# A search of three bits a step, two dense tiles and scattered results in a layer of experts that choose

## The chip, the cores and the metric

The kernel runs on one core of one Trainium2 chip. A core has a matrix engine (TensorE, PE in the profile, with its weight loads as PEld), a vector engine (VectorE, DVE), an activation engine (ScalarE, ACT), a general engine (GpSimd, POOL), and a synchronisation engine (SyncE, SP) that issues most DMAs; ACT and POOL issue DMAs too. Each engine works through its own queue in order, and queues wait for each other by semaphores. The metric is device time in microseconds (us). Three runs of the kernel before took 3548.22, 3555.48 and 3563.23; the median is 3555.48.

## The reference

A decoder of four levels, each with an attention, a cross attention with a context and a feed-forward part, works on x, 2048 tokens (16 batches of 128) of 256 values. Every part is `x = x + part(layernorm(x))`. The change touches the feed-forward part of level 2, in which 8 experts choose their tokens, and the end of the loop that three cross attentions share.

```python
def _L2_ffn_ref(x, Wg, W1, W2):          # E = 8, T = 2048, cap = T // E = 256
    logits = xt @ Wg
    probs = jax.nn.softmax(logits, axis=-1)
    pT = probs.T
    _, top_idx = jax.lax.top_k(pT, cap)
    sel = jnp.zeros((E, T), dtype=bool).at[jnp.arange(E)[:, None], top_idx].set(True)
    masked = jnp.where(sel, pT, -jnp.inf)
    assigned = sel.any(axis=0)
    tok2exp = jnp.where(assigned, jnp.argmax(masked, axis=0), jnp.argmax(pT, axis=0))
    weights = jnp.take_along_axis(probs, tok2exp[:, None], axis=1)[:, 0]
    out = jnp.zeros_like(xt)
    for e in range(E):
        gate = jnp.where(tok2exp == e, weights, 0.0)
        h = jax.nn.gelu(xt @ W1[e], approximate=False) @ W2[e]
        out = out + gate[:, None] * h
    return out.reshape(B, S, D)
```

Each expert takes its 256 likeliest tokens; a token goes to the likeliest of the experts that took it, or, if none did, to the likeliest of all. So every token has exactly one expert, and the number of an expert's tokens depends on the data. W1[e] is 256x512 and W2[e] 512x256, 512 KB each.

## The kernel before

x lies in SBUF as 16 tiles of 128 tokens, four groups of four (`self.x[g][:, t, :]`). The parts run one after the other. A list scheduler places most instructions; those that go through `pinned`, `pinned_transpose` (L255 to L260) or `keep_in_program_order` keep the order in which the program states them on PE. So PE's order around the change is written by hand. PSUM tiles come from `b1` (one bank, four buffers) and `b2` (two banks, two buffers).

**Cross attention** (`xattn64`, for L1, L2 and L3). Its loop (L1230 to L1248) is a pipeline over units, 16 of them in L2. Turn m runs the sums d of unit m-1, the scores st of unit m, the values o of unit m-1, whose normalising product rb (PE) is copied by ACT (L1213) and multiplied in by DVE into cT (L1215), and then the output projection of unit m-2 (`project`, L1218), which `add_x` (L222) adds to x. Level 2 hands in a dictionary `beside` of work for single turns: it comes from `l2_ffn_begin` (L1850 to L1912), which also prepares DRAM rows and SBUF tiles. From turn 10 on it lays the statistics, the normalised rows ("hall") and the logits of group after group beside the attention. The logits of a group are two products per half with the gate weights wg as the stationary operand, 32 columns of which 8 are used, and 512 tokens moving ("lT", 32x512). The work of the last group (`st["last"]`) is left for `l2_ffn`.

**Experts** (`l2_ffn`, L1914 to L2168). In order:

- tail: group 3's statistics, rows, transposes, logits; the lT of all groups is turned back, softmax over 8 logits gives p (128x16x8), one transpose gives pT, 128x128, in which partition (tile, expert) holds 128 tokens' probabilities;
- search (L1994 to L2003): the 256th largest probability of each expert, as the bits of a float32, two bits in each of 15 steps. DVE makes three candidates, compares pT with each in an instruction that also sums its mask, PE adds up over the 16 partitions of an expert ("count"), DVE keeps the largest candidate that at least 256 tokens reach;
- ranks (`ranks`, L2008 to L2017): which tokens are above or at the threshold, each token's expert, its place `at` among the expert's tokens (L2071), the expert of every block of 128 places (`ebi`). Experts fill up to 16 + 7 = 23 blocks, each with tokens of one expert;
- moves (L2086 to L2093): 16 indirect DMAs by POOL write the rows of a tile to their places in DRAM `hs`, which was filled with zeros long before;
- blocks (L2150 to L2161): 23 blocks, two stages deep. `fetch` (L2098) reads rows (ACT's queue, after the moves; block 0 alone, then four at once) and, on SP, the block's weights by a register that holds the expert; weights use one of 7 slots of 8 KB per partition that the whole program shares (`slot`, L118). `tokens` transposes the rows ("htr"), `first_product` (tokens stationary, 512 columns of W1 moving, then gelu on ACT), `turn` transposes the result ("ytr", DVE copy), `second_product` (256 columns of W2 moving), whose result yo (two buffers) ACT copies and sends to DRAM `ys`;
- return (L2162 to L2168): 16 indirect DMAs by POOL gather each token's row of ys, and DVE adds it, times the gate, to x.

Then `l3_attn` (L2172) begins with the layernorm of group 0.

Of the kernel before, what the change touches and what calls it, by code (L numbers as in the profile page):

```python
# [17 lines left out]
P = 128  # L18
B = 16
# [11 lines left out]
class Decoder:  # L31
# [1052 lines left out]
    def xattn64(self, H, names, bias, tag, begin=None):  # L1084
# [12 lines left out]
        with self.tc.tile_pool(name=tag, bufs=1) as wk:  # L1097
# [132 lines left out]
            for m in range(N + 2):  # L1230
                if 0 < m <= N:
                    r = sums(es[m - 1])
# [10 lines left out]
                if m > 1:  # L1243
                    project(*units[m - 2], cTs.pop(m - 2))
# [605 lines left out]
    def l2_ffn_begin(self):  # L1850


        nc = self.nc
        E = 8
        wg = self.wp.tile([P, 2, 32], F, tag="wg2", name="wg2")
        nc.gpsimd.memset(wg, 0.0)
        nc.sync.dma_start(out=wg[:, :, 0:E], in_=self.a["L2_ffn_Wg"].rearrange("(c p) n -> p c n", p=P))
        zero = self.hp.tile([P, DM], F, tag="hT", name="zero", bufs=5)
        nc.gpsimd.memset(zero, 0.0)
        NB = B + E - 1  # L1860
        hs = self.tc.dram_tile([NB * P, DM], F, name="hs")
        for b in range(NB):
            nc.sync.dma_start(out=hs[b * P : (b + 1) * P, :], in_=zero)
        h = [self.slot([P, 8, DM], "hall") for _ in range(2)]
        st = {"hs": hs, "h": h}
        self.l2f = st
        vals = {}

        def stats(gs):
            n = len(gs)  # L1870
            bs = self.small([P, GB, 6], "bnst")
            mv = self.small([P, n, GB, 2], "l1mv")
            rs = self.small([P, n, GB], "l1rs")
            for i, g in enumerate(gs):
                for t in range(GB):
                    nc.vector.bn_stats(bs[:, t, :], self.x[g][:, t, :])
                    nc.vector.bn_aggr(mv[:, i, t, :], bs[:, t, :])
            self.rsqrt(rs, mv[:, :, :, 1])
            for i, g in enumerate(gs):
                vals[g] = mv[:, i], rs[:, i]  # L1880

        def rows(g):
            mv, rs = vals[g]
            for t in range(GB):
                nc.vector.tensor_scalar(
                    h[g // 2][:, g % 2 * GB + t, :], self.x[g][:, t, :], mv[:, t, 0:1], rs[:, t : t + 1], ALU.subtract, ALU.mult
                )

        def logits(g):
            hT = self.hp.tile([P, 2, GT], F, tag="hT", name="hT", bufs=5)  # L1890
            for k in range(2):
                ps = self.b1("tr")
                for t in range(GB):
                    self.pinned_transpose(ps[:, t * P : (t + 1) * P], h[g // 2][:, g % 2 * GB + t, k * P : (k + 1) * P])
                self.evac(hT[:, k, :], ps)
            r = slice(32 * g, 32 * g + 32)
            ps = self.b1("lT")
            for k in range(2):
                self.pinned(ps[r, :], wg[:, k, :], hT[:, k, :], start=k == 0, stop=k == 1)
            if g == 0:  # L1900
                st["lT"] = self.hp.tile([P, GT], F, tag="h", name="lT", bufs=2)
            nc.scalar.copy(st["lT"][r, :], ps[r, :])

        st["last"] = [lambda: stats([3]), lambda: rows(3), lambda: logits(3)]
        at = lambda f, *a: lambda: f(*a)
        return {
            10: [at(stats, [0, 1]), at(rows, 0)],
            11: [at(rows, 1), at(logits, 0)],
            12: [at(logits, 1)],
            14: [at(stats, [2]), at(rows, 2)],  # L1910
            15: [at(logits, 2)],
        }  # L1912

    def l2_ffn(self):  # L1914

        nc = self.nc
        E, CAP = 8, T // 8
        NB = B + E - 1  # L1920
# [3 lines left out]
        with self.tc.tile_pool(name="l2f", bufs=1) as wk:  # L1924
# [7 lines left out]
            for i in range(15):  # L1932
                for j in range(3):
                    nc.gpsimd.memset(bits[:, i, j : j + 1], (j + 1) << (2 * i))
# [738 lines left out]
```

## Time and profile before

| what | value |
|---|---|
| median of three runs | 3555.48 us |
| profiled execution | 3552.78 us, span 3551.1 us |
| PE busy | 3291.6 us (93%), 20930 instructions |
| DVE busy | 2121.4 us (60%) |
| ACT busy | 1416.5 us (40%) |
| POOL busy | 418.6 us (12%) |
| mean granted PE clock | 0.967 |
| chain that ended last | PE 79%, DVE 10%, ACT 5%, issue 3% |
| weights of blocks, 46 DMAs of 512 KB | 5.0 us from issue to landing |

Everything in the profile is one execution. Its page divides the span in 40 equal slices of 88.8 us; a digit is a busy share in tenths, and "PEclk" is the clock that the throttle granted to PE, in tenths of full speed. The windows of the trace give the same for chosen stretches: busy time of each engine with the number of instructions in parentheses, the clock, the share of the 16 DMA engines, and GB/s. A timeline line has start, duration, engine, line of the program, operation, output<-input with shapes, how many were taken together, and in brackets the idle time before and what ended it. "ACTq" and "SPq" are DMA issues on these queues. "at+5" below means 5 us after the cast that makes `at` ended (2246.4).

### The profile page before, as it was taken

The numbers are of one execution on the slowest core, as the hardware profiler recorded it, in microseconds if no ns is written. First come the engines' busy times: TensorE is split into PE (matmuls) and PEld (weight loads), VectorE is DVE, ScalarE is ACT, GpSimd is POOL, SyncE is SP. The second block draws the span as 40 slices with busy tenths as digits, with TensorE's granted clock in tenths as the row PEclk, the third lists the DMA queues.
The fourth block names the chain that finished last, engine by engine and source line by source line (L and its number), as shares of the span: only waits on it lengthen the run. The fifth ranks groups of instructions, "written<-read, shape, count | busy, mean of one in ns | idle before, by whom it ended". The sixth has DMA issues, their size and how long they took to land.

```text
span 3551.1 us, 51415 instructions
## 1 busy us (share of the span) xinstructions
PE 3291.6 (93%) x20930; PEld 1776.4 (50%) x20947; DVE 2121.4 (60%) x4215; ACT 1416.5 (40%) x1896; POOL 418.6 (12%) x603
## 2 busy tenths in 40 slices
PE   7999999999999999998999997478999999999999
PEld 4656655555566566664555564352222222225656
DVE  5546444444565545477777544336999989954430
ACT  2357111111124322247555222024677767783221
POOL 5410000000003310110000210113000000002100
PEclk9989999999999999999999998687999999999989
DMA  2000000000010100010100000655102020000000
GB/s 79 1 23 15 18 18 18 22 19 18 29 50 2 38 1 1 1 43 13 42 1 13 2 1 1 216 177 135 25 12 32 12 32 11 11 1 26 1 8 18
DMA packets 90500, 105.46 MB, mean 30 GB/s; under 512 B 11380, under 2 KB 72694, under 8 KB 90006
## 3 DMA queue, kind: packets, MB, share of 16 engines
q1 hardware_dynamic: 79672, 89.71, 9.8%
q0 software_dynamic: 4224, 6.43, 0.6%
q10 hardware_dynamic: 6368, 6.03, 0.5%
q8 instruction: 165, 2.70, 0.3%
q14 instruction: 71, 0.58, 0.1%
HBM read 85.53 MB, written 16.60 MB: 29 GB/s over the span
## 4 chain that ended last, share of the span: by engine, by line
PE 79%; DVE 10%; ACT 5%; issue 3%; DMA 1%; POOL 1%; POOLq 0%; DVEq 0%; ACTq 0%
PE acc L2205 7%; PE down L257 7%; PE gate L257 6%; PE up L257 6%; PE proj L257 6%; PE st L2205 5%; PE one L2205 4%; PE st L257 4%; PE qT L168 4%; PE h L257 2%; PE o L257 2%; DVE mx L2351 2%; PE rb L257 2%; PE v L1113 2%; PE fc L168 2%
## 5 line engine op out<-in xcount | busy, mean ns | idle before, releaser
L2351 DVE TENSOR_REDUCE mx<-one 128x1 f32<-128x512 f32 x1024 | 658.4, 686 | 59.0 <-PE one L2205 50.0
L2488 ACT ACTIVATE e<-st 128x1024 f32<-128x1024 f32 x512 | 497.1, 1021 | 209.6 <-PE st L2205 208.5
L803 ACT ACTIVATE gs<-gate,cols 128x512 f32<-128x512 f32 x132 | 90.7, 687 | 551.3 <-PE gate L257 544.3
L2205 PE MATMUL acc<-e,v 128*32 128x512 f32 x2048 | 285.6, 612 | 0.9 <-ACT e L2488 0.9
L817 DVE SCALAR_TENSOR_TENSOR x<-down,w_all,x 128x256 f32<-128x256 f32 x512 | 212.4, 477 | 110.4 <-PE down L257 110.2
L2205 PE MATMUL st<-qp,kp 113*128 113x512 bf16 x1024 | 272.4, 386 | 6.0 <-DMA qp<-shifts 3.7
L257 PE MATMUL down<-expert,gs 128*128 128x256 f32 x1056 | 249.4, 379 | 2.2 <-DVE gs L804 2.2
L257 PE MATMUL gate<-hT,expert 128*128 128x512 f32 x528 | 248.5, 593 | 0.2 <-ACT hT L712 0.2
L257 PE MATMUL up<-hT,expert 128*128 128x512 f32 x528 | 248.1, 592 | 0.0
L257 PEld LDWEIGHTS down<-expert,gs 128*128 128x128 f32 x1056 | 200.6, 190 | 85.7 <-issue 61.5
L804 DVE SCALAR_TENSOR_TENSOR gs<-up,cols,gs 128x512 f32<-128x512 f32 x132 | 99.0, 750 | 228.6 <-PE up L257 227.7
L2205 PE MATMUL one<-kp,qp 16*128 16x512 bf16 x1024 | 211.3, 396 | 3.7 <-DVE mx L2351 2.4
L2205 PEld LDWEIGHTS <-qp 16*128 16x128 bf16 x1024 | 48.8, 91 | 327.4 <-issue 322.1
L257 PEld LDWEIGHTS up<-hT,expert 128*128 128x128 f32 x528 | 100.3, 190 | 126.3 <-issue 126.3
L2205 PEld LDWEIGHTS <-kp 113*128 113x128 bf16 x1024 | 79.0, 98 | 143.9 <-issue 82.5
L1213 ACT COPY rb<-rb 128x512 f32<-128x512 f32 x64 | 37.5, 585 | 259.7 <-PE rb L257 259.7
L1215 DVE TENSOR_TENSOR cT<-o,rb 128x512 f32<-128x512 f32 x64 | 44.2, 691 | 151.8 <-ACT rb L1213 151.8
L257 PEld LDWEIGHTS gate<-hT,expert 128*128 128x128 f32 x528 | 99.6, 190 | 70.3 <-issue 63.5
L168 PE MATMUL qT<-hT,L_xattn_Wq 128*128 128x512 f32 x256 | 114.1, 599 | 4.8 <-DVE hT L112 4.8
L257 PE MATMUL o<-e,v 128*32 128x128 f32 (+1 forms) x2048 | 104.6, 277 | 12.6 <-DVE nm L294 11.8
L1524 DVE SCALAR_TENSOR_TENSOR xs<-xBC,cols,xs 128x508 f32<-128x508 f32 x144 | 106.0, 741 | 12.3 <-ACT xs L1520 9.0
L257 PEld LDWEIGHTS o<-e,v 128*32 128x32 f32 (+1 forms) x2048 | 80.9, 123 | 28.4 <-POOL e L335 12.3
(539 smaller groups left out, 5371.2 us busy)
## 6 DMA issues: line engine op xcount, KB each, us to landing
W<-in_L_ffn_W_dram SPq DMA_DIRECT2D x46, 512.0 KB, 5.0
expert<-in_L_ffn_Wg_dram SPq DMA_DIRECT2D x32, 128.0 KB, 2.2
expert<-in_L_ffn_Wu_dram SPq DMA_DIRECT2D x32, 128.0 KB, 2.4
expert<-in_L_ffn_Wd_dram SPq DMA_DIRECT2D x32, 128.0 KB, 2.4
parts<-parts SPq DMA_DIRECT2D x16, 256.0 KB, 2.4
qp<-parts SPq DMA_DIRECT2D x28, 128.0 KB, 3.8
kp<-parts SPq DMA_DIRECT2D x12, 256.0 KB, 8.3
hs<-zero SPq DMA_DIRECT2D x23, 128.0 KB, 1.9
```

The source lines that it names most:

```text
L168: self.nc.tensor.matmul(out, lhsT, rhs, start=i == 0, stop=i == n - 1 and bias is None)
L257: self.tc.keep_in_program_order(self.nc.tensor.matmul(*a, **k))
L803: nc.scalar.activation(gs, pg, AF.Silu, bias=bg)
L804: nc.vector.scalar_tensor_tensor(gs, pu, bu, gs, ALU.add, ALU.mult)
L817: nc.vector.scalar_tensor_tensor(xt, pd[:, t, :], w_all[:, o : o + 1], xt, ALU.mult, ALU.add)
L1113: nc.tensor.matmul(ps, l, r, start=True, stop=False)
L1213: nc.scalar.copy(rb, ps)
L1215: nc.vector.tensor_tensor(cT, po, rb, ALU.mult)
L1524: stt = lambda *a: pin(nc.vector.scalar_tensor_tensor(*a))
L2205: self.tc.keep_in_program_order(nc.tensor.matmul(*a, **k))
L2351: nc.vector.tensor_reduce(mx[:, t, kc, i : i + 1], pair[i], AX.X, ALU.max)
L2488: nc.scalar.activation(e[:, 2 * p : 2 * p + 2, :], ps, AF.Exp, scale=1.0 / 16.0)
```

## The change

What it does, part by part:

1. In the shared loop of the cross attentions, turn N (the first without new scores) now runs the projection of unit N-2 ahead of the sums of unit N-1 instead of behind its values.
2. Logits are made by tile: the transposed tokens are the stationary operand and the 8 columns of wg move, so the result has tokens on partitions and isn't turned back. Maxima and subtraction follow per call, softmax per group. Group 2 and tiles 12 to 14 are done in turns 13 to 16 beside the attention; tile 15 alone is left. A small Exp, kept in program order, stands ahead of the tail's softmax.
3. The search takes three bits in each of 10 steps. Probabilities lie eight times in pT (128x1024; a partition is one expert, one of two halves of the tiles and one of eight candidates), made by copies and eight transposes. A step has one comparison with a sum over 1024 columns, with a candidate of its own in each partition; PE's one product with "same" gives the eight counts to every partition of the expert.
4. Tiles 0 and 1 are not moved: all 8 experts' products are made for them ("dense", tokens 2x128 moving, weights stationary), in 64 pieces of two matmuls. `fill(n)` states n pieces at that place in PE's order: 3 in the tail, 2 in each step, 1 behind the threshold, 1 in each `ranks`, 4 between, and the rest behind the moves. Their weights are loaded ahead of the blocks' and use the same slots. DVE adds each expert's result to x, times the gate or zero.
5. So 14 tiles are moved, and 14 + 7 = 21 blocks are made. Rows have a 257th value, the token's number, and hs's padding rows get numbers from 2048 on.
6. `second_product` no longer issues a plain write on ACT: POOL scatters yo by the token numbers to rows of ys in token order. The return is then four plain loads on SP and 14 additions.

```diff
             for m in range(N + 2):
+                if m == N:
+                    project(*units[m - 2], cTs.pop(m - 2))
                 if 0 < m <= N:
                     r = sums(es[m - 1])
...
-                if m > 1:
+                if m > 1 and m != N:
                     project(*units[m - 2], cTs.pop(m - 2))
...
-        wg = self.wp.tile([P, 2, 32], F, tag="wg2", name="wg2")
+        wg = self.wp.tile([P, 2, E], F, tag="wg2", name="wg2")
...
-        NB = B + E - 1
+        W = DM + 1
+        NB = B - 2 + E - 1
...
+            for i in range(10):
+                nc.vector.tensor_scalar(bits[:, 8 * i : 8 * i + 8], j8, float(1 << (3 * i)), None, ALU.mult)
+                nc.vector.tensor_scalar(own[:, i : i + 1], mine[:, 0:1], float(1 << (3 * i)), None, ALU.mult)
...
-            ps = self.b1("lT")
-            for k in range(2):
-                self.pinned(ps[r, :], wg[:, k, :], hT[:, k, :], start=k == 0, stop=k == 1)
+            ps = self.b1("logits")[:, 0 : n * E]
+            for i in range(n):
+                for k in range(2):
+                    self.pinned(ps[:, i * E : (i + 1) * E], hT[:, k, S(i)], wg[:, k, :], start=k == 0, stop=k == 1)
...
-        st["last"] = [lambda: stats([3]), lambda: rows(3), lambda: logits(3)]
+        st["last"] = [lambda: stats([15]), table, lambda: rows([15]), lambda: logits([15]), lambda: softmax(3)]
         at = lambda f, *a: lambda: f(*a)
         return {
-            10: [at(stats, [0, 1]), at(rows, 0)],
-            11: [at(rows, 1), at(logits, 0)],
-            12: [at(logits, 1)],
-            14: [at(stats, [2]), at(rows, 2)],
-            15: [at(logits, 2)],
+            10: [tables, at(stats, G(0, 1)), at(rows, G(0))],
+            11: [at(rows, G(1)), at(logits, G(0))],
+            12: [at(logits, G(1)), at(softmax, 0)],
+            13: [at(stats, G(2)), at(softmax, 1), at(rows, G(2))],
+            14: [at(logits, G(2))],
+            15: [at(softmax, 2)],
+            16: [at(stats, [12, 13, 14]), at(rows, [12, 13, 14]), at(logits, [12, 13, 14])],
         }
...
+                def second(e, w2, yT):
+                    po = self.b1("yd")
+                    for t in range(2):
+                        for c in range(4):
+                            self.pinned(
+                                po[:, t * DM : (t + 1) * DM], yT[:, c, S(t)], w2[:, c, :], start=c == 0, stop=c == 3
+                            )
+                            if c % 2:
+                                if t and c == 3:
+                                    nc.scalar.copy(yd[:, e, :], po)
+                                yield
+                last = None
+                for e in range(E):
+                    w1, w2 = weights(e)
+                    ps = self.b2("h1d").rearrange("p (c n) -> p c n", c=4)
+                    for c in range(4):
+                        for k in range(2):
+                            self.pinned(ps[:, c, :], w1[:, k, S(c)], hT[:, k, 0 : 2 * P], start=k == 0, stop=k == 1)
+                        if c < 3:
+                            yield
+                    yT = tile_([P, 4, 2 * P], "yTd", bufs=2)
+                    nc.scalar.activation(yT, ps, AF.Gelu)
+                    yield
+                    if last:
+                        yield from second(*last)
+                    last = e, w2, yT
+                yield from second(*last)
...
+            for g in (0, 2, 1):
+                copied(g)
+            turned(0)
+            copied(3)
+            fill(3)
+            turned(1)
...
-            for i in range(14, -1, -1):
-                nc.vector.tensor_tensor(cand, bits[:, i], thr.bitcast(I32).to_broadcast([P, 3]), ALU.bitwise_or)
-                for j in range(3):
-                    nc.vector.tensor_scalar(
-                        mask, pT, cand.bitcast(F)[:, j : j + 1], 0.0, ALU.is_ge, ALU.add, accum_out=count[:, j : j + 1]
-                    )
-                ps = self.b1("count")[:, 0:3]
-                self.pinned(ps, flat(same), count, start=True, stop=True)
-                nc.vector.scalar_tensor_tensor(best[:, 0:3], ps, CAP - 0.5, cand.bitcast(F), ALU.is_ge, ALU.mult)
+            for i in range(9, -1, -1):
+                b8 = slice(8 * i, 8 * i + 8)
...
+                    nc.vector.tensor_tensor(own, f["own"][:, i : i + 1], thr.bitcast(I32), ALU.bitwise_or)
+                nc.vector.tensor_scalar(mask, pT, own.bitcast(F), 0.0, ALU.is_ge, ALU.add, accum_out=count)
+                nc.vector.tensor_scalar(counts, f["pick"], count, None, ALU.mult)
+                if i < 9:
+                    nc.vector.tensor_tensor(all8, f["bits"][:, b8], thr.bitcast(I32).to_broadcast([P, 8]), ALU.bitwise_or)
+                ps = self.b1("count")[:, 0:8]
+                products(ps, [(f["same"], counts)])
+                fill(2)
+                nc.vector.scalar_tensor_tensor(best, ps, CAP - 0.5, all8.bitcast(F), ALU.is_ge, ALU.mult)
                 nc.vector.tensor_reduce(thr, best, AX.X, ALU.max)
...
-            for t in range(B):
-                i = nc.gpsimd.indirect_dma_start(
-                    hs[:, :], bass.IndirectOffsetOnAxis(ap=at[:, t : t + 1], axis=0), h[t // 8][:, t % 8, :], None
-                )
+            for t in range(2, B):
...
+            fill(64)
+            w2 = tile_([P, 2, E], "w2")
+            self.tc.keep_in_program_order(
+                nc.vector.tensor_tensor(w2, oh[:, 0:2, :], gate[:, 0:2].unsqueeze(2).to_broadcast([P, 2, E]), ALU.mult)
+            )
+            for e in range(E):
+                for t in range(2):
+                    xt = self.x[0][:, t, :]
+                    nc.vector.scalar_tensor_tensor(
+                        xt, yd[:, e, t * DM : (t + 1) * DM], w2[:, t, e : e + 1], xt, ALU.mult, ALU.add
+                    )
...
-                nc.scalar.dma_start(out=ys[b * P : (b + 1) * P, :], in_=yo)
+                ids = hbs[-(-b // 4)][:, (b - 1) % 4 if b else 0, DM:W].bitcast(U32)
+                i = nc.gpsimd.indirect_dma_start(ys[:, :], bass.IndirectOffsetOnAxis(ap=ids, axis=0), yo, None)
+                each(backs, i)
...
-            for t in range(B):
-                back = wk.tile([P, DM], F, tag="back", name="back", bufs=4)
-                nc.gpsimd.indirect_dma_start(
-                    back, None, ys[:, :], bass.IndirectOffsetOnAxis(ap=at[:, t : t + 1], axis=0)
-                )
-                xt = self.x[t // GB][:, t % GB, :]
-                nc.vector.scalar_tensor_tensor(xt, back, gate[:, t : t + 1], xt, ALU.mult, ALU.add)
+            for g in range(NG):
+                t0 = 0 if g else 2
+                back = wk.tile([P, GB, W], F, tag="hb", name="back", bufs=3)[:, :, 0:DM]
+                nc.sync.dma_start(
+                    out=back[:, t0:, :],
+                    in_=ys[(g * GB + t0) * P : (g + 1) * GT, :].rearrange("(t p) d -> p t d", p=P),
+                )
+                for t in range(t0, GB):
+                    xt = self.x[g][:, t, :]
+                    n = g * GB + t
+                    nc.vector.scalar_tensor_tensor(xt, back[:, t, :], gate[:, n : n + 1], xt, ALU.mult, ALU.add)
```

## The prediction

> **What bounds the kernel now.** I read the page's slices first, then the stage by windows, then its stretches instruction by instruction. TensorE (PE) is busy for 93% of the span. One place is not like that, slices 26 to 28, the L2 ffn (2184 to 2397 us), and the change is made there:
>
> ```profile
> PE   7999999999999999998999997478999999999999
> ...
> PEclk9989999999999999999999998687999999999989
> ```
>
> The digits to see are "7478" in PE and, below them, "8687": there PE idles and its clock falls.
>
> ```profile
> core 0: us, PE busy (x) PEld busy (x) DVE busy (x) ACT busy (x) POOL busy (x), PEclk, DMA share, GB/s
> 2200.00:2235.00 35.00, 8.77 (x30) 7.31 (x31) 22.30 (x130) 0.00 (x0) 0.00 (x0) 0.50 0.00 0
> 2247.00:2260.00 13.00, 0.00 (x0) 0.00 (x0) 0.00 (x0) 0.00 (x0) 9.96 (x11) 0.50 0.92 314
> 2290.00:2310.00 20.00, 20.00 (x88) 13.70 (x87) 5.58 (x10) 4.51 (x10) 0.00 (x0) 1.00 0.99 312
> 2372.00:2400.00 28.00, 8.30 (x19) 3.72 (x20) 16.81 (x56) 3.31 (x7) 16.26 (x19) 0.57 0.27 79
> ```
>
> Four stretches with four limits: the search (a chain of DVE and PE, DMA unused), the moves of rows (POOL and DMA), the blocks (PE full), the return (POOL). One search step:
>
> ```profile
> 2204.88 0.16 DVE L2002 SCALAR_TENSOR_TENSOR best<-count,cand 128x3 f32<-128x3 f32 x1 [0.74 <-PE count L257]
> 2205.07 0.16 DVE L2003 TENSOR_REDUCE best<-best 128x1 f32<-128x4 f32 x1
> 2205.26 0.16 DVE L1995 TENSOR_TENSOR cand<-bits,best 128x3 int32<-128x3 int32 x1
> 2205.46 0.35 DVE L1997 TENSOR_SCALAR_CACHE_REDUCE mask<-pT,cand 128x128 bf16<-128x128 f32 x1
> ...
> 2206.51 0.08 DVE L1997 DVE_READ_ACCUMULATOR mask<-pT,cand 128x1 f32 x1
> 2206.65 0.59 PE L257 MATMUL count<-count,same 128*128 128x3 f32 x2 [1.81 <-DVE mask L1997]
> 2207.28 0.16 DVE L2002 SCALAR_TENSOR_TENSOR best<-count,cand 128x3 f32<-128x3 f32 x1 [0.68 <-PE count L257]
> ```
>
> From one "best" to the next: 2.40 us, 15 times, 2198.14 to 2234.08. Small DVE operations stand .2 apart, the three masks .39 each. Then rows move:
>
> ```profile
> 2266.03 0.96 POOL L2088 DMA_INDIRECT hs<-hall,at  x1 [0.30 <-issue]
> ...
> 2269.17 3.24 ACTq L2103 DMA_DIRECT2D hb<-hs  x4
> 2271.31 0.29 PEld L260 LDWEIGHTS htr<-ident,hb 128*128 128x128 f32 x2 [28.32 <-issue]
> ...
> 2272.53 3.78 PE L257 MATMUL h<-W,hTs 128*128 128x512 f32 x4 [0.52 <-DVE hTs L2123]
> ```
>
> The sixteenth move starts 19.6 us after the ranks (`at`, 2246.4), the first block is read when it has landed, and its products run at half clock (3.78 for four; 1.73 later). Blocks (the chain of waits) are PE alone, 4.10 each, x8 and x4 being the two products:
>
> ```profile
> 2304.10 0.22 PE htr L260 x2
> 2304.32 1.73 PE h L257 x8
> 2306.05 0.44 PE ytr L260 x4
> 2306.48 1.72 PE h L257 x4
> ```
>
> Last product 2370.59, sixteen gathers at 1.25 from 2373.80, last x 2395.87, first product of l3_attn 2393.67.
>
> **The change, part by part.** The sum is made against the profiled execution: 3552.78 (span 3551.1 and 1.7 outside), 2.7 below the median 3555.48. The bound of 0.5% is 17.8 us.
>
> *1. project(N-2) ahead of sums(N-1), in L1, L2, L3.* In before the last rb is followed by project(N-2), which covers ACT's rb copy (.59) and DVE's cT (.69). After, only project(N-1) is left behind them: PE waits 1.3 plus hand-overs, and the x addition of N-2 (.42) now precedes the reciprocal r in DVE's queue. Moved work costs nothing itself. L1 and L3 have nothing else for that gap: +1.5 each (0, if the earlier additions bring the next stage forward, to 2). In L2 the transposes and logits of tiles 12 to 14 fill it; project(15) now stands behind them.
>
> *2. Logits by tile, softmax by group.* A group's two matmuls 128x512 (an f32 matmul leaves two records; four, 1.73) become eight with 8 columns; the nearest row is rb, 128x128, eight records in 1.16, so sixteen in 2.3. Between -.5 and +1.3 a group, as weight loads decide. The added DVE work (tables: 20 small operations at .17, two reductions .38, 4.6 us in unit 10; softmax per group 1.1) fits in DVE's idle half (2128 to 2135: 1.38 busy of 7), but stands ahead of other units' operations: taken +1.5 for the stage, range -.5 to +4. The tail, 2184.65 to the first mask at 2198.14, loses three of four rows (1.05), lT (3.28, half clock), its copy, and the table load (1.28); it starts about 2 later, behind the logits of 12 to 14, and adds per tile products, three copies before and one after (.42 each), six dense products ahead of the second set of transposes (2.6; 5.1 at half clock), and a pT copy of .69. I count 10 to 12.5 from 2186.4, so the first mask comes at 2198.2: 0 (-2 to +3.4).
>
> *3. Search.* A step is own, one mask over 1024 columns, counts, count product, best, reduce; the all8 operation lies beside the product. This mask form at 1024 is in no row. Its row at 128 is .346; 896 further elements at one a cycle (.96 GHz, as TENSOR_REDUCE and TENSOR_TENSOR, .686 at 512 against .29 at 128, show: 1.03 ns each) make 1.28. The lower end is the plain TENSOR_SCALAR, .685 at 1024, and .13 for the difference at 128 (.346 against .219): .81. Upper end: .346 taken as all streaming but .06, 2.3. I take 1.28, since the form's own row is nearest to one a cycle. Step: .6 for three small operations, 1.42 mask with its read, .2 counts, .35 product and wait: 2.6; PE's two dense pieces (four products at .43, 1.73) fit inside. Ten steps, the first at half clock: 26.5 for 36.0, **-9.5** (-14.2 to +4).
>
> The Trainium skill, "VectorE: DVE Perf Modes", The perf-mode tier table, says that fp32 tensor_scalar in SBUF reaches two elements a cycle. The plain rows agree (128x2048 in 1.22 to 1.29), and by it the mask would be .81 and the sum 5 lower; no row shows it for the accumulating form.
>
> *4. Ranks.* One pieces group, and w2 plus an x update (.29, .48) before `at`: +.8 (0 to 2).
>
> *5. Dense work beside the moves.* Eight experts times eight pieces of two products 128x256: 128 x .43 = 55 us. Thirty pieces go before `at`, 34 (29.2 us) are left, against a cover from `at` to the first block of 24.9 in before; two moves fewer make that 22.4. ACT issues hb0 after gelu 5, and this issue waits for all moves; the copies and gelus 6 and 7 queue behind it. 26 of the 34 pieces need none of these (22.4 us from the second ranks, 4 ahead of `at`), so PE stops about `at`+18.4. The moves land at 20.2 (19.6 less two at 1.26, and 3.12); one copy (.6), three issues (.35) and a gelu (1.0) later, at 23.2, the last eight pieces begin, 6.9 and some 1.7 for half clock: 31.8; block 0's second product comes at `at`+37.5 for 33.3: **+4.2** (-2, if PE gets ahead in the search; +8, if more pieces run at half clock). DVE's 16 updates of x (.48 each, 7.7) fit beside. SP loads the dense weights while DMA stands at 0.00 in the search; bout (landed 1992, used with 4.3 us to spare) waits behind two of these loads, at most 3.4. Zeros' extra column of 4-byte elements and the POOL iotas lie before 1728, with Wv waiting on a buffer until 1909. These are costed at nothing.
>
> *6. Blocks.* 21 for 23: **-8.2**. Their bytes per block (1 MB of weights, .26 of rows) take 4.1 at 312 GB/s, as long as PE; before had 25 us of lead, of which 20 were left at the end (DMA share .14 from 2350). After: about 12 of lead; range -8.2 to 0.
>
> *7. Return.* yo goes by indirect scatter on POOL; after the last, 3.9 (.35 to start, and the last move's 3.12 to land), then four plain loads of 1.84 MB (5.9 at 312 GB/s), 14 updates. Last x at +14.5 for +25.3. But in DVE's new order l3's first h follows all updates: first l3 product about +18.3 for +23.1: **-5** (-2 to -8).
>
> Sum: 1.5 + 1.5 + 1.5 + 0 - 9.5 + .8 + 4.2 - 8.2 - 5 = -13.2, so **3540**.
>
> **Rivals.** *A, mask at two elements a cycle:* plain rows speak for it, .346 against it. Search -14.2: 3535; with the return at its better end 3532.
> *B, search at half clock:* pieces 4 x .85 + .57 = 4.0 a step, 40 us: 3553. For it: from 2439 to 2481 the clock stays .50 with PE 73 to 94% busy. Against: from 1569 to 1575 it stays 1.00 with PE 43% busy, and in such steps PE would be full. The Trainium skill, "TensorE: Matmul & The Clock Gate", What's actually happening, asks about 3.4 us of sustained work to get the full clock; by it the first step or two alone would be slow. Block 0 needs about 4.5 (2272.5 to 2277), in agreement.
> *C, slower: the scatter paces the blocks.* yo has two buffers. Its copy, .35 and the landing L must stay within 8.2 + 1.8 (ACT's idle before the next gelu): L up to 9.2. Moves landed in 5.7, at most 6.8, the last in 3.1; a W load took up to 10.0. Beyond 9.2, half the excess is paid in 19 blocks; from L = 12.5 on the kernel is slower by the bound: L = 13 gives 3576.
> *D, the dense work doesn't go beside the search:* count products queue behind pieces that wait for gelu (128x1024, 1.02) in four steps: +5, 3545. Against: a gelu's result is used four pieces later.
>
> **How the numbers follow.** Forecast .50 (own range 3526 to 3553), A .20, B .17, C .06, D .07. Faster: .17 of A and a third of the forecast, .34. Slower: C and a little of B, .07. Same .59. Eight in ten reach from 3518 (A with good ends of 5 and 7) to 3560 (B with the poor end of the tail and a search of 4 per step).
>
> **What will show it.** The mask's duration (1.28 or .81); step 2.6; PEclk 1.00 in the search; 34 dense pieces after `at` with a hole of about 5 us that ends at ACT's hb issue; blocks of 4.10 with yo scatters landing under 8; last x 14 us after the last product; rb followed by a wait at the ends of L1 and L3. The prediction falls if the clock stays low through the search, if POOL's scatters pace PE, or if the mask is far from 1.28.

## The result: no measurable change, where 0.4% was forecast

| | before | after |
|---|---|---|
| median of 20 runs each | 3554.52 us | 3550.14 us |
| lowest and highest | 3540.79 to 3563.31 | 3541.12 to 3564.06 |
| profiled execution | 3552.78 us | 3564.06 us |

The ratio after to before is 0.9994, with a 95% interval of 0.9981 to 1.0006: about 2 us less by the ratio and 4.4 by the medians, and within the bound of 0.5%. The time is inside the range, but the forecast gain of 13 us (0.4%) wasn't there. The profiled execution of after is the longest of its 20. Most of that lies behind the changed code, as is seen below.

Each stage is measured between starts or ends of instructions that both programs have (us). "Forecast" and "measured" are differences to before:

| stage | before | after | forecast | measured |
|---|---|---|---|---|
| end of L1's cross attention (first hTb to first gy) | 35.98 | 39.36 | +1.5 | +3.38 |
| L2 attention and tail (last kT copy to first mask) | 75.78 | 84.82 | +1.5 | +9.04 |
| search (first mask to end of the last reduction) | 35.89 | 27.23 | -9.5 | -8.66 |
| ranks (to the end of the cast of `at`) | 12.37 | 13.17 | +.8 | +.80 |
| moves and dense rest (to block 0's second product) | 33.14 | 39.77 | +4.2 | +6.63 |
| blocks (to the last product's end) | 91.06 | 85.53 | -8.2 | -5.53 |
| return (to l3_attn's first product) | 23.08 | 17.70 | -5 | -5.38 |
| end of L3's cross attention | 9.23 | 10.97 | +1.5 | +1.74 |
| sum | 316.53 | 318.55 | -13.2 | +2.02 |

The span of after is 11.3 us longer, so 9.3 of it fall in code that the change doesn't touch. One place has more than all of it: from l3_attn's first product to its 151st maximum ("mx") it is 159.67 us for 144.86. PE's clock is at half there in both, and stays so for longer in after (the rest of the untouched code is 5.5 shorter). Windows of after, then of before (PE busy with its instructions, PEld, DVE, ACT, POOL, granted clock, DMA share, GB/s):

```profile
2437.50:2512.60 75.10, 68.09 (x151) 12.39 (x150) 46.89 (x76) 24.46 (x28) 22.20 (x15) 0.50 0.61 124
```

```profile
2434.30:2482.10 47.80, 43.07 (x84) 7.92 (x83) 30.86 (x52) 17.59 (x21) 22.02 (x14) 0.50 0.77 171
```

PE is busy for 91% and 90% of the two, yet the clock is .50 over 75.1 us in one and 47.8 in the other. Such spells add up to 34 to 75 us there in the profiles of the kernels here, in one to three pieces, so a stage table is safer than two spans.

Where 11 us of the forecast went, the stages say. In the experiment e4 below, whose code is that of after up to the blocks, the touched stages together are 2.2 below before, as the ratio has it. Against the forecast of -13.2 they lack 11.0: .2 and .3 at the ends of L1 and L3, 4.5 in the tail of L2, .8 in the search, 2.6 beside the moves, 3.0 in the blocks; the return gives .4 back.

The page of after, 40 slices, PE and its granted clock:

```profile
PE   7999999999999999998999998978999999999989
...
PEclk9989999999999999999999998986899999999989
```

Where before had "7478" over "8687", the same four slices (25 to 28; the prediction's "26 to 28" is one off) now read "8978" over "8986"; the last of them and the 8 behind it hold the spell in l3_attn. By windows:

```profile
2210.00:2240.00 30.00, 24.33 (x106) 18.88 (x107) 21.35 (x72) 5.53 (x6) 0.00 (x0) 0.94 0.21 68
2247.00:2260.00 13.00, 12.78 (x61) 11.28 (x61) 6.18 (x27) 2.63 (x3) 6.94 (x7) 1.00 0.51 169
2260.00:2272.00 12.00, 9.99 (x47) 8.45 (x45) 0.00 (x0) 0.00 (x0) 6.84 (x8) 1.00 0.63 195
2272.00:2290.00 18.00, 14.11 (x47) 10.27 (x48) 5.92 (x15) 4.78 (x7) 0.00 (x0) 0.81 0.97 327
```

The search (first row) runs at a mean clock of .94, with PE busy for 24.3 of 30. From 2247 to 2260, where PE was idle, it is full. In the third row ACT and DVE do nothing for 12 us: that is the hole of step 5. One search step:

```profile
2224.18 0.17 DVE L2119 SCALAR_TENSOR_TENSOR best<-count,cand 128x8 f32<-128x8 f32 x1 [0.48 <-PE count L257]
...
2224.77 1.28 DVE L2112 TENSOR_SCALAR_CACHE_REDUCE mask<-pT,cand 128x1024 bf16<-128x1024 f32 x1
...
2226.38 0.39 PE L257 MATMUL count<-counts,pr 128*128 128x8 f32 x2 [0.41 <-DVE counts L2113]
...
2226.81 0.17 DVE L2119 SCALAR_TENSOR_TENSOR best<-count,cand 128x8 f32<-128x8 f32 x1 [0.48 <-PE count L257]
```

Best to best is 2.63, the mask 1.28. The hole beside the moves:

```profile
2266.37 3.62 PE L257 MATMUL h1d<-hTd,W 128*128 128x256 f32 x16
...
2268.01 0.96 POOL L2217 DMA_INDIRECT hs<-hall,at  x1 [0.30 <-issue]
2272.31 0.35 ACTq L2244 DMA_DIRECT2D hb<-hs  x1
2272.70 0.58 ACT L2037 COPY yd<-yd 128x512 f32<-128x512 f32 x1 [15.41 <-DMA hs<-hall,at]
...
2273.83 1.02 ACT L2050 ACTIVATE yTd<-h1d 128x1024 f32<-128x1024 f32 x1 [0.54 <-ACT yd L2037]
...
2274.91 9.93 PE L257 MATMUL yd<-W,yTd 128*128 128x256 f32 x32 [4.92 <-ACT yTd L2050]
```

ACT stood for 15.41 us behind its own DMA issue, which waited for the last move; copy and gelu came behind it, and PE had 4.92 us without work. The end of L1:

```profile
1565.98 0.69 DVE L1215 TENSOR_TENSOR cT<-o,rb 128x512 f32<-128x512 f32 x1 [1.83 <-ACT rb L1213]
...
1566.72 3.41 PE L257 MATMUL proj<-L_xattn_Wo,cT 128*128 128x256 f32 x8 [1.40 <-DVE cT L1215]
```

The wait is the one foreseen (1.40). But the eight products take 3.41, and 1.99 in the profiles where the clock doesn't fall here. The tail of L2 on PE:

```profile
2192.72 2.77 PE L257 MATMUL logits<-wg,hT 128*128 128x8 f32 x12
2195.34 3.58 PE L257 MATMUL proj<-L_xattn_Wout,cT 128*128 128x256 f32 x8
...
2204.31 5.00 PE L257 MATMUL h1d<-hTd,W 128*128 128x256 f32 x12
```

Tile 15's projection stands behind the logits of tiles 12 to 14, both at half clock, and the dense pieces between the two sets of transposes of pT take 5.00. The return:

```profile
2386.00 3.24 DVE L2306 SCALAR_TENSOR_TENSOR x<-back,gate,x 128x256 f32<-128x256 f32 x8
...
2389.62 1.81 DVE L207 TENSOR_SCALAR h<-x,bnmv,rstd 128x256 f32<-128x256 f32 x4
...
2393.91 3.78 PE L2343 MATMUL pT<-hT,L_proj_wT 128*128 128x512 f32 x4 [1.10 <-ACT hT L2410]
```

Plain loads (issued from 2379.60) take the place of the gathers, and l3's first h does stand behind all additions.

### The profile page after: what moved, and what is told of

Its sections match the earlier page's. It is cut to its first block, busy times and chain, and to the rows that moved or that the text cites. A ratio compares the mean times of both kernels' runs of the same rounds, so it can differ in the third digit from the quotient of the medians.

```text
span 3562.3 us, 51927 instructions
## 1 busy us (share of the span) xinstructions
PE 3355.7 (94%) x21208; PEld 1830.1 (51%) x21208; DVE 2124.6 (60%) x4205; ACT 1425.3 (40%) x1908; POOL 421.6 (12%) x565
## 5 line engine op out<-in xcount | busy, mean ns | idle before, releaser
L257 PE MATMUL o<-e,v 128*32 128x128 f32 (+1 forms) x2048 | 105.8, 279 | 12.6 <-DVE nm L294 11.8
L257 PE MATMUL proj<-L_xattn_Wo,cT 128*128 128x256 f32 x384 | 96.7, 396 | 2.8 <-DVE cT L1215 2.8
```

Of the source, the lines that this page charges most:

```text
L257: self.tc.keep_in_program_order(self.nc.tensor.matmul(*a, **k))
```

## The experiments

Four questions were left by the table: what the ends of L1 and L3 cost, and whether order or clock; what makes the tail 4.5 to 7.5 dearer; whether the hole and the blocks' loss come from ACT's row issues or from the two yo buffers; and whether the dense part pays at all. For the tail the theory at first was that the logits of tiles 12 to 14 delay the last projection, with the three dense pieces and the new order as rivals; the clock came in as a second theory when the first profiles were compared. Unless said otherwise an edit is to the kernel after, and computes the same.

**e1: the order at the ends of the cross attentions**

```diff
-                if m == N:
-                    project(*units[m - 2], cTs.pop(m - 2))
...
-                if m > 1 and m != N:
+                if m > 1:
```

> The changed kernel with project(N-2) back behind the values of unit N-1, in all three cross attentions. Theory A (the earlier projection takes away PE's cover, and the uncovered 1.4 us wait also drops PE's clock for the window after it): the end of L1's cross attention comes back by 3.8 us (gy at the time of before, +0.0 to -0.5 against it), that of L3 by 1.7, the half-clock window at 1567 is gone. In L2, where the gap holds the logits of tiles 12 to 14: x of tile 14 is later by 2 to 4, and the first mask moves by -1 to +2. Rival B (the 3.8 is the tail of work that moved, not the order): L1 comes back by 1.5 at most and the half-clock window stays.

The end of L1 took 35.99 and that of L3 9.30, where after had 39.36 and 10.97: both are back at before's values (35.98, 9.23). In the six profiles below that keep the new order and lose no clock there, L1 took 37.67. So the order costs 1.7 at each end, and the other 1.7 of L1 in after were the clock. The tail of L2 stayed at 84.25: the reordering is not what ails it. The stage between L1 and L2's tail was 3 longer (556.26 for 553.06), with half-clock windows elsewhere; such a gain or loss of a window is the noise under all single stages here.

So what the old order is worth to the whole time isn't shown. In the four kernels that have it in L1 and the rest of the change (e1, c1, c2, g2) this untouched stage took 554.8 to 556.3, and 553.0 to 554.8 in the eight with the new order: L1's end and this stage together take 590.7 to 592.3 for 591.2 to 592.5. Before, with the old order too, took 553.08 there (589.06 together) with two half-clock windows, where e1 had six.

**e2: dense pieces out of the tail**

```diff
             copied(3)
-            fill(3)
             turned(1)
```

> The changed kernel without the three dense pieces between the two sets of transposes in the tail; they are made later, behind the moves. Theory A (they stand at half clock on the path to the first mask: from the end of the first pT product at 2204.3 to the second at 2209.15): first mask 4.0 to 4.6 us earlier; the dense work's stop behind ACT's row read shrinks from 4.9 to 2.4 because three more pieces (2.6) fill it, and block 0 comes 4 to 4.6 earlier too. Rival B (the path to the mask is the softmax of group 3 and its copy, and the clock is set by other gaps): first mask at most 2 earlier. Rival C: the mask comes earlier, but the pieces are added whole behind the moves, so that block 0 comes only 1.5 to 2 earlier.

The first mask came after 79.24, for 81.8 to 84.8 in kernels with the same tail: 2.5 to 5.6 earlier. Block 0 came 1.7 later and the search took .5 more. So about 2.3 of the gain were paid back behind the tail: the three pieces then ran after `at`. How much is left, 0 to 3, lies within the noise of a stage.

**e3: rows read on SP's queue**, issued after the block's weights:

```diff
+                e = nc.sync.value_load(ebi[0:1, b : b + 1], min_val=0, max_val=E - 1)
+                ws[b] = weights(e)
...
-                    nc.scalar.dma_start(
+                    nc.sync.dma_start(
...
-                e = nc.sync.value_load(ebi[0:1, b : b + 1], min_val=0, max_val=E - 1)
-                ws[b] = weights(e)
```

> The changed kernel with the reads of block rows (hb) issued by SP, behind the block's weights, not by ACT. Theory A (ACT's issue of the first read waits for all moves, and dense copies and gelus queue behind it): PE's 4.9 us wait for gelu goes, the dense work ends about 5 us earlier, 28.9 behind the cast of at instead of 33.8, block 0's second product at +34.5 to 35.5 instead of 39.8; and the wait of ACT's yo copy in the first blocks (3.3 us) goes. Rival B (the moves themselves hold block 0 and 1, by rows or by the weights of block 1 whose slot they free): the dense work ends 5 earlier, but block 0 or 1 then waits, and the last product comes at most 2 earlier.

Timeline of this kernel (`at` ends at 2244.63):

```profile
2263.54 7.07 PE L257 MATMUL yd<-W,yTd 128*128 128x256 f32 x32
...
2267.07 0.82 SPq L2246 DMA_DIRECT2D hb<-hs  x2
...
2270.44 0.38 PE L260 MATMUL htr<-ident,hb 128*128 128x128 f32 x2
```

The last dense products stand without a wait and take 7.07 for 9.93, at full clock: after had two half-clock windows from 2273.7, behind its hole, and this kernel has none there. Dense work ends at `at`+26.0 for +33.9. Block 0's second product came after 31.82 for 39.77: 8.0 less, below before's 33.14. And the blocks took 82.85 for 85.53, which is the -8.2 of the forecast to the digit. Moving the row reads, one line of the program, returns 10.6 us in these two stages, four fifths of what the whole change was to bring. (The edit changes the queue and puts the reads behind the block's weights; the two weren't tried apart.)

**e4: four yo buffers for two**

```diff
-                 yo = wk.tile([P, DM], F, tag="yo", name="yo", bufs=2)
+                 yo = wk.tile([P, DM], F, tag="yo", name="yo", bufs=4)
```

> The changed kernel with four yo buffers instead of two. Theory A (scatters of 2.4 to 7.5 us are paid in blocks only through the two buffers): the waits of PE for yo (1.8 us) go, blocks take 4.10 each: from block 0's second product to the last 82 us instead of 83.5. Rival B (rows' buffers hb, held by the scatter because the token numbers lie in them, make ACT wait in its issue of the next rows): 1 us or less is gained, the 3.3 us wait on ACT stays.

The blocks took 85.84: no gain. ACT's queue, in after and then here:

```profile
2298.27 0.37 ACTq L2244 DMA_DIRECT2D hb<-hs  x1
...
2298.68 0.37 ACT L2279 COPY yo<-h 128x256 f32<-128x256 f32 x1 [3.26 <-DMA ys<-yo,hb]
```

```profile
2288.91 0.37 ACTq L2244 DMA_DIRECT2D hb<-hs  x1
2289.32 0.37 ACT L2279 COPY yo<-h 128x256 f32<-128x256 f32 x1 [3.11 <-DMA ys<-yo,hb]
```

The row "waits for ys<-yo,hb" looks like a yo buffer, but directly ahead of it is a row issue. The token numbers by which a block is scattered lie in its hb, so hb is held until the scatter has landed, and the issue that refills it stops ACT. With four yo buffers the wait stands as before (3.11); with the issue on SP, PE has no wait for yo left. Scatters landed in 2.4 to 7.5 us, median 5.0, under the 9.2 at which the two yo buffers alone would have paced the blocks.

**f1: logits of tiles 12 to 14 behind the last projection**

```diff
-            16: [at(stats, [12, 13, 14]), at(rows, [12, 13, 14]), at(logits, [12, 13, 14])],
+            16: [at(stats, [12, 13, 14]), at(rows, [12, 13, 14])],
+            17: [at(logits, [12, 13, 14])],
```

> The changed kernel with one edit: the transposes and logits of tiles 12 to 14 stand behind project(15) in PE's order, not ahead of it. Theory A (the way from L2's last scores to the first mask is longer because project(15) and all of tile 15's work queue behind these skinny products, which PE runs at half clock): x of tile 15 comes 4 to 5 us earlier, the first mask 3 to 4 earlier (L2's last kT copy to first mask about 78 instead of 82 to 85; before 75.8). Rival B (the way is set by the copies, dense pieces and transposes that follow tile 15): x of tile 15 earlier, but the first mask less than 1.5 earlier.

```profile
2179.25 1.99 PE L257 MATMUL proj<-L_xattn_Wout,cT 128*128 128x256 f32 x8 [1.46 <-DVE cT L1215]
...
2187.00 4.44 PE L257 MATMUL h1d<-hTd,W 128*128 128x256 f32 x12
```

The tail took 75.56, 9.3 less than after and level with before (75.78). From the last kT copy to the addition of x(15) it was 64.2, for 73.3 in after and 61.9 in before. The projection runs at full clock, 3.9 behind the start of unit 15's values for 8.3. So the order on PE made the delay. Part of the 9.3 is clock: e2 and e4, which have no half-clock window ahead of 2182, as f1 hasn't, reach x(15) after 70.16, so that the order alone is worth about 6.0.

**f2: the same, with three dense pieces ahead of tile 15's transposes**

```diff
-            for work in f["last"]:
+            for i, work in enumerate(f["last"]):
+                if i == 3:
+                    fill(3)
...
-            fill(3)
```

> As the last one, and the tail's three dense pieces stand ahead of tile 15's transposes, where PE waits 2.7 us for its normalised row, instead of between the two sets of transposes. Theory A: they are hidden there and keep PE's clock up; L2's last kT copy to first mask 74.5 to 76.5, another 2 to 4 less than with the logits moved alone, and block 0 isn't put off (the cast of at to block 0's second product stays within 0.5 of 39.8). Rival B (weights of expert 0 come too late, or half clock makes the pieces longer than the wait): no gain, or a loss of up to 2.

The tail took 77.78, but with two half-clock windows (3.4 us from 2142 and from 2152) that f1 didn't have, before anything that differs. From x(15) to the first mask it took 10.53 for 11.36: the edit itself is worth .8, not 2 to 4.

**g1: logits with 64 columns for 8**, the gate weights read eight times over by a stride of zero, of which the first eight results are used:

```diff
-            ps = self.b1("logits")[:, 0 : n * E]
+            ps = self.b1("logits")[:, 0 : n * 64]
+            wide = lambda k: wg[:, k, :].unsqueeze(1).to_broadcast([P, 8, E])
...
-                    self.pinned(ps[:, i * E : (i + 1) * E], hT[:, k, S(i)], wg[:, k, :], start=k == 0, stop=k == 1)
+                    self.pinned(ps[:, i * 64 : (i + 1) * 64].rearrange("p (r e) -> p r e", e=E), hT[:, k, S(i)], wide(k), start=k == 0, stop=k == 1)
```

> The changed kernel with one edit: the 8 gate columns stand eight times side by side in the moving operand of the logits products (64 columns, read by a stride of zero; one copy of the result is used). Theory A (PE's clock for the next 3.4 us is set by how many columns pass through how much of the array in a window, and the 8-column products count for next to nothing though PE is occupied all the time): weight loads keep the pitch at 0.13 us a record, so the logits take the same 2.1 a group; no half-clock window begins between L2's last kT copy and the transposes of tiles 12 to 14 (2119 to 2180), whatever the window's position; in the ten profiles so far the windows with fewer than about 1,500 of 8,192 weighted columns fall, and none of these windows is left below 1,800. L2's last kT copy to its last x addition: 70 or less. Rival B (the clock falls for the short waits around the logits): half-clock windows after the logits remain in this stretch, as in five of ten profiles before. Rival C: 64 columns make the products longer, 3 us or more a group.

Windows of 3.4 us in the L2 attention, after and then this kernel, at the same phase of the clock:

```profile
2147.40:2150.80 3.40, 3.23 (x43) 2.98 (x45) 1.54 (x6) 0.68 (x2) 0.00 (x0) 1.00 0.00 0
2150.80:2154.20 3.40, 3.40 (x29) 2.85 (x26) 0.43 (x1) 0.00 (x0) 0.00 (x0) 0.50 0.00 0
```

```profile
2147.50:2150.90 3.40, 3.07 (x40) 2.78 (x42) 1.50 (x6) 0.81 (x2) 0.00 (x0) 1.00 0.00 0
2150.90:2154.30 3.40, 3.40 (x54) 2.99 (x50) 0.63 (x1) 0.50 (x2) 0.00 (x0) 1.00 0.02 5
```

```profile
2147.83 2.10 PE L257 MATMUL logits<-wg,hTd 128*128 128x64 f32 x16 [0.35 <-DVE hTd L112]
```

In after PE is 95% busy from 2147.4 (3.23 of 3.40), with the 8-column logits in it, and in the next window its clock is halved: 29 records for 54. With 64 columns PE is no busier (3.07) and the clock stays. The wider groups cost next to nothing: 2.10 to 2.16 for 2.06 to 2.11, so the moving columns don't set their time; that the loads of the stationary tokens do is likely, but not shown. The tail took 81.57 for 84.82, and last kT to x(15) 70.08 for 73.3, just above what was expected. These times alone wouldn't show it, since e2 and e4 took 70.16 with narrow logits: of the ten profiles with 8 columns seven have half-clock windows between the last kT and 2182, of the two with 64 none has.

**d0: no dense part**, all 16 tiles moved, 23 blocks, search and scatter as in after:

```diff
-        NB = B - 2 + E - 1
+        NB = B + E - 1
...
-            pieces = dense()
+            pieces = iter(())
...
-            D = B - 2
+            D = B
...
-            for t in range(2, B):
+            for t in range(B):
```

> The changed kernel without its dense part: all 16 tiles are moved, 23 blocks are made, no pieces stand in the tail, in the search or behind the moves; all else as changed. Theory A (the dense tiles save two blocks of 4.1 and two moves, but their overhang behind ACT's read of rows costs 6.6, and in the search they keep PE's clock up): search 28 to 29 (27.2), the cast of at to block 0's second product 32.5 to 34.5 (39.8), blocks 22 x 4.1 = 91 to 94 (85.5): the three together within 2.5 of the changed kernel's 165.7 (with at's chain). First mask 2 to 5 earlier, since no pieces stand in the tail. Rival B (the dense part pays as it stands): 5 or more longer in sum. Rival C (half clock makes no difference to the search): search 27.2.

```profile
2195.00:2230.00 35.00, 9.37 (x34) 7.50 (x34) 23.16 (x78) 1.13 (x3) 0.00 (x0) 0.51 0.00 1
```

With PE idle again the search falls to half clock (.51) and still takes only 28.37 for 27.23. Moves to block 0 took 36.84, blocks 94.30, return 22.32. From the first mask to the last product that is 171.9 (28.37 + 12.39 + 36.84 + 94.30), for 165.7 in after: the dense part pays 6.2 there, and hole and all it is no loss in these stages, as rival B had it. (The whole time of this single run, 3547.18, is inside after's own range and decides nothing.) (The return is 4.6 longer without it, too: two more additions, and l3's first h 3.7 after the last of them.) The first mask didn't come earlier for the pieces that are missing (82.29).

**c1: two edits together**, e3 and the new order in L2 alone:

```diff
-                if m == N:
+                if m == N and tag == "l2x":
...
-                if m > 1 and m != N:
+                if m > 1 and (m != N or tag != "l2x"):
```

> The changed kernel with two parts undone together: project(N-2) in its old place in L1 and L3 (L2 keeps the new one), and block rows read by SP. Theory A (the losses are independent): ends of L1 and L3 as before, the cast of at to block 0's second product 31.8, blocks 82.9; in sum 5.4 and 10.6 off the changed kernel, about 16 us, 3534 where the changed kernel has 3550: 0.5% faster than before, ratio 0.994 to 0.997. Rival B (a shorter stage is given back by the clock in L3's attention, which stays low longer or shorter with its arrival): ratio 0.998 to 1.001 in spite of the shorter stages.

3535.53 for 3553.36, ratio 0.9967 (0.9944 to 0.999; 0.9950 by the medians). The ends of L1 and L3 are back at 35.98 and 9.15, block 0 at 32.88 and the blocks at 82.85, so the two edits add up in these stages; the stage behind L1 took 556.26, so that nothing of L1's gain is left there.

**c2: all together**, c1, f1, f2, no pieces in the last search step and three behind the threshold, `at`'s cast kept in program order, and l3's first layernorm stated ahead of the later additions:

```diff
-                fill(2)
+                fill(2 if i else 0)
...
-            fill(1)
+            fill(3)
...
-            nc.vector.tensor_copy(at[:, 2:], m[:, 2:])
+            self.tc.keep_in_program_order(nc.vector.tensor_copy(at[:, 2:], m[:, 2:]))
...
+                if g == 0:
+                    self.h0 = self.layernorm(0)
...
-                h = self.layernorm(g)
+                h = self.layernorm(g) if g else self.h0
```

> As c1_two, with the logits of 12 to 14 behind project(15), the tail's pieces ahead of tile 15's transposes, no dense pieces in the last search step (three behind the threshold's transpose instead of one), at's cast kept ahead of the x updates, and L3's first normalisation ahead of the x updates of groups 1 to 3. Theory A: first mask 75 to 76.5 behind the last kT copy, threshold to at 12.2 to 12.6 (13.2 in the changed kernel, 1.3 of them a wait of the threshold's transpose for two pieces), last product to L3's first product 13.5 to 14.5 (17.7); 25 to 30 us off the changed kernel, 3521 to 3526, ratio 0.990 to 0.993. Rival B (clock in L3's attention gives it back): ratio 0.995 or more.

3528.56 for 3553.36, ratio 0.9924 (0.9901 to 0.9948). The return fell to 14.10, as expected. The ranks did not: 13.48, where 12.2 to 12.6 were expected, so the order of the pieces and the cast were not what costs there; what does was not settled. The tail took 79.15 for 75 to 76.5, with three half-clock windows in it.

**g2: all together with the 64 columns**, the edits of c2 and of g1:

> As c2_all (old order in L1 and L3, rows read by SP, logits of 12 to 14 behind project(15), tail pieces ahead of tile 15, last search step free, cast and first normalisation ahead), with the widened logits. Theory A: the half-clock windows that c2_all had in the approach to the search (three, 1.6 each) are gone: L2's last kT copy to first mask 73 to 75 (79.2), the later stages as in c2_all; 3 to 5 us less than c2_all, 3521 to 3526 against a before of 3553, ratio 0.990 to 0.993. Rival B (the clock windows only move elsewhere): no less than c2_all, 0.9924 or more.

3522.06 for 3552.46, ratio 0.9919 (0.9888 to 0.9951): faster than both kernels (its longest run, 3538.22, is below the shortest of after, 3541.12). The tail took 74.46 with no half-clock window from 2120 to 2189, the return 14.01:

```profile
2359.22 0.46 DVE L2309 SCALAR_TENSOR_TENSOR x<-back,gate,x 128x256 f32<-128x256 f32 x1
2359.60 1.38 DVE L207 TENSOR_SCALAR h<-x,bnmv,rstd 128x256 f32<-128x256 f32 x4
```

The first h now stands among the additions. The intervals of c2 and g2 overlap, so the 64 columns are shown by their windows, not by the whole time.

## Why the prediction was right and wrong

1. *Order at L1 and L3, +1.5 each.* Right in mechanism and size for these stages (1.40 of wait, 1.7 in all by e1). The further 1.7 in L1 of the profiled execution is a window at half clock, which the step didn't price.
2. *Logits by tile, +1.5, and the tail, 0.* This failed most: +6.0 in e4 and +9.0 in after. The duration of a group was near (2.06 to 2.11 for "about 2.3"). The step said of project(15) that it "now stands behind" the logits of tiles 12 to 14, in part 1, and then gave no price for that, because "the transposes and logits of tiles 12 to 14 fill it". They fill the gap of cT, but they wait for the rows of three tiles themselves, and everything behind needs x(15). f1 puts the price at 9.3 against after and 6.2 against e4, whose clock was like its own up to 2182: that is the whole excess of e4. The second thing missed is that products of 8 columns can let the clock fall while PE counts as busy: g1 shows it at two places of one profile, about 1.6 each.
3. *Search, -9.5.* Measured -8.66, mask 1.28 and step 2.63 as worked out. Seven of the nine intervals between masks are 2.62 to 2.69; the .84 are one step of 3.46, the second, whose count product stood behind two dense pieces at half clock (3.49). The forecast put only the first step at half clock and its pieces beside it at nothing. Rival A (a mask of .81) falls with it. The Trainium skill, "SBUF — State Buffer", Who interferes with whom, excepts the form of tensor_scalar that also writes its accumulator from the two-port modes; the row (1.28 for 1024 elements against .346 for 128, 1.04 ns an element) agrees, and the tier table that the prediction cited doesn't make the exception.
4. *Ranks, +.8.* +.80.
5. *Dense work beside the moves, +4.2.* The chain was right link by link: PE stopped at `at`+19.1 (18.4), went on at +24.0 (23.2), ended at +33.9 (31.8). The last move took 4.3 to land, not 3.12 as in before, and the last eight pieces lost 3.0 to the clock, not 1.7. That makes most of the +6.63. (The prediction's own terms from the landing to the restart add up to 22.9, not 23.2.) The wait itself was foreseen, and e3 shows that it goes when the row reads leave ACT's queue.
6. *Blocks, -8.2.* Measured -5.53, within the range. The step looked at the weights' bytes and at yo's buffers; the 2.7 were paid for hb, which the new scatter holds longer and whose refill stands in ACT's queue. Rival C's mechanism, a scatter that holds up ACT, was at work through another buffer and at less than a tenth of its price. e3 has -8.2.
7. *Return, -5.* -5.38, first l3 product +17.7 for "+18.3". The loads began 3.4 after the last product (the prediction wrote 3.9, though its terms .35 and 3.12 make 3.5), and the last x was done at +13.0 for "+14.5".

Rival B (search at half clock) did not occur: after the second step the clock stayed full; without the pieces it is .51. Rival D (counts behind pieces) occurred in that one step, for .8 of its 5. The sum failed by two costs that were left at nothing, project(15) behind the logits in step 2 (4.5 above its 1.5) and ACT's later row reads in step 6 (2.7), and by a term that was seen and underpriced, step 5 (2.4). The time stayed in the range since these are a few us each, not because the terms were right: -13 was forecast and about -2 came.

## What to carry to other kernels

Before a DMA issue is left on an engine that also computes, list what the issue waits for and what is queued behind it: here one such issue held ACT for 15.4 us, and moving it and those of the later blocks to SP's queue returned 10.6 us. When side work is laid into an engine's fixed order, price it by what is placed behind it, not by its own duration, and keep it behind the last product that the next stage needs. Where a profile's clock row drops with PE busy, look at how narrow the products are.

## What the runs showed of the hardware that was not expected

The clock doesn't follow PE's busy share. Changes of the granted clock lie on a grid of 3.413 us in every profile. For each window of that grid in 13 profiles of this study, the records of products that start in it were added up, each with its moving columns times the share of the 128 by 128 array that it uses (a float32 product leaves two records). The window of after from 2147.4 comes to 1,408 (logits 128, d 512, st 768), and in g1 to 2,048 (1,024, 512, 512). How often the next window was granted the other clock:

| weight of a window | at full clock, then falls | at half clock, then rises |
|---|---|---|
| under 1,280 | 137 of 139 | 5 of 357 |
| 1,280 to 1,535 | 24 of 29 | 5 of 52 |
| 1,536 to 1,791 | 18 of 74 | 42 of 110 |
| 1,792 to 2,047 | 8 of 94 | 55 of 58 |
| 2,048 to 2,559 | 4 of 470 | 70 of 82 |
| 2,560 and more | 4 of 11,928 | 6 of 11 |

The border lies near 1,500 to 1,800, in both directions. It isn't the whole rule: about one in six of the half-clock windows above 2,048 stayed at half clock. It fits the long spell of l3_attn in after, where PE is busy for nine tenths with products of 16 rows among others: its windows weigh 256 to 1,728, but for the last two (2,320 and 2,192), and full clock follows them. That the chip counts by just this weight is inferred from the table; g1 is the one test of it by an edit. The Trainium skill, "TensorE: Matmul & The Clock Gate", HAM oscillation, puts the rule as no idle gaps of PE above some 3.4 us; the window's length agrees (3.413), and the window from 2147.4, 95% busy and followed by half clock, shows that the absence of idle time isn't enough.
